# Moving a division to GpSimd, a second buffer for v and a new order of loads in a fused four-layer kernel

## The chip, the cores and the metric

The kernel runs on one core of a Trainium2 chip, as one program with one launch. The time is the device time of that program in microseconds (us). Before the change three runs took 3732.04, 3734.66 and 3744.95 us; the median, 3734.66 us, is what the change is measured against. The profile is of one further execution, whose span is 3730.0 us.

The core has five engines with their own in-order streams of instructions: TensorE (PE in the profile, its weight loads PEld), VectorE (DVE), ScalarE (ACT), GpSimd (POOL) and SyncE (SP), which issues most of the transfers here.[...]

## The reference, cut to what matters

Four layers follow each other on x of 4 images, 256 channels, 48 x 48 points, float32; each adds its result to x after a group norm. Layer 0 is an attention-weighted sum over 49 dilated taps, layers 1 and 2 are 3 x 3 convolutions with binarised and ternary weights. The change touches layer 3, a linear attention over square windows of three sizes:

```python
q = sigmoid(einsum('bchw,oc->bohw', x, Wq))        # 8 heads of 32 channels
k = sigmoid(einsum('bchw,oc->bohw', x, Wk))
v = einsum('bchw,oc->bohw', x, Wv)
v = v / maximum(norm(v, axis=1), 1e-12)            # per head
Ik, Ikv = integral(k), integral(k (x) v)           # two-dimensional running sums
for w in (1, 2, 4):                                # windows of 48, 24, 12 points
    wk, wkv = box(Ik, 48 // w), box(Ikv, 48 // w)  # sums over the window
    attn = einsum('bdhw,bdfhw->bfhw', q, wkv)
    norm = einsum('bdhw,bdhw->bhw', q, wk)
    outs.append(attn / (norm + 1e-6))              # <- the division
out = einsum('bchw,oc->bohw', concatenate(outs), Wout) + bout
```

## The kernel before

Layer 3 does not use running sums for `wkv`. It works in blocks: an image b, one half of the heads ct (four heads of 32 channels are 128 partitions) and eight rows of queries rb. Six row blocks, two halves and four images make 48 blocks, counted i = 0 to 47 in the order image, half, row block. A block goes over tiles of keys (a row block a, a third of the columns c): TensorE makes the scores of a tile, VectorE, ScalarE and GpSimd copy them out of PSUM under the masks of the three windows, and two tiles later TensorE adds up scores times v.

```python
LAG = 2
stream = [(i, a, c, ...) for i, (b, ct, rb) in enumerate(order) for n, (a, c) in enumerate(tiles_of(rb))]
for n in range(len(stream) + LAG):
    if n < len(stream):                       # tile n
        if at == 0: begun(i)
        ss = [blocks[i].scores(pr, a, c) for pr in range(NPR)]
        ahead.append(blocks[i].masked(a, c, ss))
        if at == 5: midway(i)                 # in the last heads: start(prepare(i))
    if n >= LAG:                              # tile n - 2
        if at == 0:
            if i >= 2: until(("done", i - 2))
            blocks[i].begin()                 # zeroes the accumulators
        for wi in (1, 0, 2): blocks[i].sums(wi, a, c, sms)
        if last: done(i)                      # finish(i) comes into turn
    advance()                                 # one step of all side jobs
```

All else runs as side jobs, Python generators that emit a few instructions at each step and say with `yield n` that they want to be called again n steps later: the next image's projections, running sums of k, norms, and the preparation and the end of blocks. The order in which they are called is the order of the instructions on each engine. `until` takes steps without emitting a tile.

```python
free = {"xr": 2, "xn": 2, "kt": 2, "sq": 2, "vt": 1, "cs": 1, "o": 1, "rc": 2, "res": 2}
FETCH = 4                                     # steps given to a transfer

def tiles_of(rb):                             # rows near rb and far ones take turns
    tiles = [(a, c) for a in sorted(range(NRB), key=lambda a: abs(a - rb)) for c in (1, 0, 2) if seen(0, a, rb)]
    near = [t for t in tiles if seen(NW - 1, t[0], rb)]
    far = [t for t in tiles if t not in near]
    both = min(len(near), len(far))
    return [t for pair in zip(near, far) for t in pair] + near[both:] + far[both:]

def prepare(i):                               # for blocks of the last heads
    yield from wait_for(("norm", b, rb))
    yield from take("o")
    o = op.tile([P, NW, NB], F32, tag="o", name="o", bufs=1)
    sync.dma_start(out=o..., in_=o_d[b][rb])  # the first heads' sums, stored earlier
    ...                                       # res: the rows of x
    for t in range(NCT):                      # one over the norms of both halves
        yield from take("rc")
        rc = op.tile([P, NW, NB], F32, tag="rc", name="rc")
        for g in range(HG):
            sync.dma_start(out=rc[g * D : (g + 1) * D]..., in_=r_d[b][rb, t * HG + g]....partition_broadcast(D))
        rcs.append(rc)
    prepared[i] = o, res, rcs

def finish(i, stage):
    yield 1
    if ct == 0:                               # first heads: store the sums
        sync.dma_start(out=o_d[b][rb], in_=stage...); made.add(("done", i)); return
    while i not in prepared: yield 1
    o, res, rcs = prepared.pop(i)
    os = (o, stage)
    for t, src in enumerate(os):              # the division, six times 128 x 384
        for wi in range(NW):
            dve.tensor_mul(src[:, wi], src[:, wi], rcs[t][:, wi])
            yield 1
        free["rc"] += 1
    for mo in range(NCT):                     # output: two accumulations on one bank
        yield from bank(2)
        ps = ps_m.tile([P, 512], F32, tag="st", name="out_ps")[:, 0:NB]
        for kt in range(NW * NCT):
            pe.matmul(ps, wout_sb[:, kt, mo * P : (mo + 1) * P], os[kt % NCT][:, kt // NCT, :], ...)
        yield 1
        dve.scalar_tensor_tensor(xs, ps, bout_sb[:, mo : mo + 1], xs, ALU.add, ALU.add)
    made.add(("done", i)); free["o"] += 1
    ...                                       # store res to the output
```

`v` of the class `Projection` makes v of one row block in three pieces, normalises it and stores it. It runs for image 0 beside image 3's layers 1 and 2, and for the other images beside the attention of the image before. The class has its tiles from a pool `scr` with two buffers for each name, unless `bufs` says otherwise:

```python
if c == 0:
    yield from take("vt")
    self.vs[g] = (self.scr.tile([P, NKC, HEADS, D], F32, tag="vt", name="vt", bufs=1), ...)
...                                           # matmuls into ps
act.copy(vt[:, c], ps)
...                                           # squares (GpSimd), sums (VectorE); for the last piece:
dve.tensor_mul(vt, vt, r...)
sync.dma_start(out=v_d[b][:, a * NKC : (a + 1) * NKC], in_=vt)
free["vt"] += 1
```

The attention stage begins with the loads for block 0; one call issues one row block of keys and one of v:

```python
qs = {0: load_q(*order[0])}
for a in range(seen_first):                   # 0, 1, 2, 3
    load_kv(0, 0, a)
```

Of the kernel before, what the change touches and what calls it, by code (L numbers as in the profile page):

```python
# [12 lines left out]
F32 = mybir.dt.float32  # L13
# [8 lines left out]
P = 128  # L22
# [52 lines left out]
HEADS, D = 8, 32  # L75
WINDOWS = (1, 2, 4)
NW = len(WINDOWS)
HALVES = [H // w // 2 for w in WINDOWS]
KC = P // RB
NKC = W // KC  # L80
# [65 lines left out]
def conv_preact_kernel(  # L146
# [53 lines left out]
    pe, dve, act, pool, sync = (  # L200
        InOrder(tc, e) for e in (nc.tensor, nc.vector, nc.scalar, nc.gpsimd, nc.sync)
    )
# [53 lines left out]
    def wait_for(*keys):  # L256
        while not made.issuperset(keys):
            yield 1

    def bank(steps):  # L260

        nonlocal bank_free
        while step < bank_free:
            yield 1
        bank_free = step + steps


    free = {"xr": 2, "xn": 2, "kt": 2, "sq": 2, "vt": 1, "cs": 1, "o": 1, "rc": 2, "res": 2}

    FETCH = 4  # L270

    def take(what):
        while free[what] == 0:
            yield 1
        free[what] -= 1
# [11 lines left out]
    class Projection:  # L287
# [84 lines left out]
        def v(self, g, a, c):  # L372
            b = self.b
            while g not in self.xn or (c > 0 and g not in self.vs):
                if g in self.left:
                    return
                yield 1
            if c == 0:
                yield from take("vt")
                self.vs[g] = (  # L380
                    self.scr.tile([P, NKC, HEADS, D], F32, tag="vt", name="vt", bufs=1),
                    self.scr.tile([P, NKC, HEADS], F32, tag="ss", name="ss"),
                )
            vt, ss = self.vs[g]
            yield from bank(1)
            ps = self.ps_tile()[:, 0:C].rearrange("p (h d) -> p h d", d=D)
            for ct in range(NCT):
                pe.matmul(
                    ps,
                    self.xn[g][:, ct, c, :],  # L390
                    proj["v"][:, ct, :],
                    start=(ct == 0),
                    stop=(ct == NCT - 1),
                )
            self.used(g)
# [3 lines that stand above are left out]
            yield from take("sq")  # L399
            sq = self.scr.tile([P, HEADS, D], F32, tag="sq", name="sq")  # L400
            pool.tensor_mul(sq, vt[:, c], vt[:, c])
            yield 2
            dve.tensor_reduce(ss[:, c, :], sq, AX.X, ALU.add)
            free["sq"] += 1
            if c < NKC - 1:
                return

            n = NKC * HEADS
            t = ss.rearrange("p k h -> p (k h)")
            r, s, u = (small.tile([P, n], F32, tag=f"{x}{n}", name=x) for x in ("vr", "vs", "vu"))  # L410
            dve.tensor_scalar_max(t, t, 1e-24)
            yield 1
            act.activation(s, t, AF.Sqrt)
            yield 1
            dve.reciprocal(r, s)
            dve.tensor_mul(u, t, r)
            dve.tensor_mul(u, u, r)
            dve.tensor_scalar(u, u, -0.5, 1.5, ALU.mult, ALU.add)
            dve.tensor_mul(r, r, u)
            dve.tensor_mul(  # L420
                vt,
                vt,
                r.rearrange("p (k h) -> p k h", h=HEADS)
                .unsqueeze(3)
                .to_broadcast([P, NKC, HEADS, D]),
# [4 lines that stand above are left out]
            made.add(("v", b, a))  # L430
# [21 lines left out]
    with (  # L452
# [26 lines left out]
        stage, owed = len(POINTS), 0.0  # L479
# [901 lines left out]
        with tc.tile_pool(name="wst", bufs=1) as wst:  # L1381
# [18 lines left out]
            for ct in range(NCT):  # L1400
                for k0, k1 in TAPS:
# [3 lines left out]
                    else:  # L1405
                        pool_, tag = {
                            (0, 0): (xp, "x1_0"),
                            (0, 2): (xp, "x1_1"),
                            (1, 0): (wst, "raw1"),
                            (1, 2): (wst, "raw"),  # L1410
                        }[ct, k0]
# [70 lines left out]
    with (  # L1482
# [179 lines left out]
        def load_q(b, ct, rb):  # L1662
            qs = qp.tile([P, RB, W], F32, tag="qs", name="qs")
            sync.dma_start(
                out=qs.rearrange("p r w -> p (r w)"),
                in_=q_d[b][ct * P : (ct + 1) * P, rb * NB : (rb + 1) * NB],
            )
            return qs
# [158 lines left out]
        def seen(wi, a, rb):  # L1827
            r0, r1 = rows_seen(wi, a, rb)
            return r0 < r1

        def tiles_of(rb):


            tiles = [
                (a, c)
                for a in sorted(range(NRB), key=lambda a: abs(a - rb))
                for c in (1, 0, 2)
                if seen(0, a, rb)
# [6 lines that stand above are left out]
        def prepare(i):  # L1845

            b, ct, rb = order[i]
# [3 lines that stand above are left out]
            sync.dma_start(out=o.rearrange("p w n -> p (w n)"), in_=o_d[b][rb])  # L1851
            yield from take("res")
            res = scr.tile([P, NCT, RB, W], F32, tag="res", name="res")
            sync.dma_start(
                out=res,
                in_=x3_d[b][:, rb * RB : (rb + 1) * RB, :].rearrange("(ct p) r w -> p ct r w", p=P),
            )
            rcs = []
            for t in range(NCT):
# [3 lines that stand above are left out]
                    sync.dma_start(  # L1863
                        out=rc[g * D : (g + 1) * D].rearrange("p w n -> p (w n)"),
                        in_=r_d[b][rb, t * HG + g]
                        .rearrange("w n -> (w n)")
                        .partition_broadcast(D),
                    )
                rcs.append(rc)
            prepared[i] = o, res, rcs  # L1870

        def finish(i, stage):


            b, ct, rb = order[i]
            yield 1
            if ct == 0:
                sync.dma_start(out=o_d[b][rb], in_=stage.rearrange("p w n -> p (w n)"))
                made.add(("done", i))
                return  # L1880
            while i not in prepared:
                yield 1
            o, res, rcs = prepared.pop(i)
            os = (o, stage)
            for t, src in enumerate(os):
                for wi in range(NW):
                    dve.tensor_mul(src[:, wi], src[:, wi], rcs[t][:, wi])
                    yield 1
                free["rc"] += 1
            for mo in range(NCT):  # L1890
                yield from bank(2)
                ps = ps_m.tile([P, 512], F32, tag="st", name="out_ps")[:, 0:NB]
                for kt in range(NW * NCT):
                    pe.matmul(
                        ps,
                        wout_sb[:, kt, mo * P : (mo + 1) * P],
                        os[kt % NCT][:, kt // NCT, :],
                        start=(kt == 0),
                        stop=(kt == NW * NCT - 1),
                    )  # L1900
                yield 1
                xs = res[:, mo].rearrange("p r w -> p (r w)")
                dve.scalar_tensor_tensor(
                    xs, ps, bout_sb[:, mo : mo + 1], xs, ALU.add, ALU.add
                )
            made.add(("done", i))
            free["o"] += 1
            yield 1
            free["res"] += 1
            sync.dma_start(  # L1910
                out=out[b, :, rb * RB : (rb + 1) * RB, :].rearrange("(ct p) r w -> p ct r w", p=P),
                in_=res,
            )

        kvs, prepared = {}, {}
# [12 lines left out]
        seen_first = HALVES[0] // RB + 1  # L1928
        until(("q", 0, 0, 0), *((what, 0, *at) for a in range(seen_first) for what, at in (("k", (0, a)), ("v", (a,)))))
        qs = {0: load_q(*order[0])}  # L1930
        for a in range(seen_first):
            load_kv(0, 0, a)


# [53 lines left out]
        for n in range(len(stream) + LAG):  # L1988
            if n < len(stream):
                i, a, c, at, last = stream[n]  # L1990
# [6 lines left out]
            if n >= LAG:  # L1997
                i, a, c, at, last = stream[n - LAG]
# [57 lines left out]
```

## Time and profile before

| | us |
|---|---|
| span of the profiled execution | 3730.0 |
| TensorE matmuls busy | 3284.1 |
| VectorE busy | 2494.9 |
| GpSimd busy | 1528.0 |
| ScalarE busy | 1067.4 |
| division of the first heads' sums, `o<-o,rc`, 72 on VectorE | 68.1 |
| division of the last heads' sums, `stage<-stage,rc`, 72 on VectorE | 58.5 |
| a multiplication of the same shape on GpSimd, `nhi<-nhi,nq` (mean of 144) | 1.055 |

Every operation is recorded through one helper line, L142, so groups are told apart by their tiles: `s` are scores, `sm` masked scores, `acc` the sums in PSUM, `stage` the sums in SBUF, `o` the first heads' sums loaded back, `rc` one over the norms, `out_ps` the output accumulation, `nhi` and `nlo` the norms' operands, `vt` v before its store, `ks` and `vs` keys and v as loaded for the attention. A row of groups gives count, busy time, mean duration and the idle time of the engine just before. A row of waits says who waited for whom, the total in us, how often, and the longest.[...] The row of a stretch of time gives its bounds and length, the busy time and number of instructions of PE, PEld, DVE, ACT and POOL, the clock granted to TensorE as a share of full speed, the DMA engines' busy share, and GB/s.

### The profile page before, as it was taken

What the parts mean: (1) busy time and instruction counts of PE and PEld (TensorE: products, weight loads), DVE (VectorE), ACT (ScalarE), POOL (GpSimd) and SP (SyncE); (2) the same over time, 40 slices, a digit from 0 to 9 for tenths busy, and PEclk for the clock granted to TensorE, in tenths of its full rate; (3) what the DMA queues carried; (4) which work ended last, traced back from release to release, by engine and by line L of the source; (5) the groups of instructions that cost most, each with busy time, mean ns of one, the idle gap of its engine ahead of it and who ended that gap; (6) DMA issues with size and microseconds to landing.
All of it is one profiled execution on the core that took longest, in us unless ns stands there. A gap on an engine that the chain in (4) does not pass through costs nothing. (4 is left out here: it accounts for less than half of the span.)

```text
span 3730.0 us, 69121 instructions
## 1 busy us (share of the span) xinstructions
PE 3284.1 (88%) x26498; PEld 1873.8 (50%) x26498; DVE 2494.9 (67%) x5059; ACT 1067.4 (29%) x2085; POOL 1528.0 (41%) x2184
## 2 busy tenths in 40 slices
PE   3689998998996788988899888999999899999998
PEld 2467686686784664433334333344444344444443
DVE  7876587586583266778667466866577866666665
ACT  0012111111114422443222334333344422333331
POOL 0000120120030024788765476866366766344442
PEclk9789999999997899999899999999999999999999
DMA  7745333324314323345344253434222444200222
GB/s 251 225 143 184 101 108 120 105 98 125 107 65 124 117 70 98 119 140 168 105 133 134 74 151 109 154 99 136 75 94 87 153 124 124 70 31 31 65 60 60
DMA packets 373020, 423.04 MB, mean 113 GB/s; under 512 B 129076, under 2 KB 328532, under 8 KB 371540
## 3 DMA queue, kind: packets, MB, share of 16 engines
q1 hardware_dynamic: 371491, 416.32, 36.2%
q8 instruction: 211, 3.46, 0.4%
q0 software_dynamic: 144, 1.52, 0.2%
q14 instruction: 118, 0.96, 0.1%
q10 hardware_dynamic: 1056, 0.79, 0.1%
HBM read 288.79 MB, written 131.25 MB: 113 GB/s over the span
## 5 line engine op out<-in xcount | busy, mean ns | idle before, releaser
L142 DVE TENSOR_TENSOR sm<-s,masks 128x112 f32<-128x112 f32 (+10 forms) x2592 | 1149.2, 492 | 704.7 <-ACT sm L142 297.1
L142 POOL TENSOR_TENSOR sm<-sm,masks 128x432 f32<-128x432 f32 (+14 forms) x1152 | 883.1, 788 | 900.9 <-ACT sm L142 397.5
L142 ACT COPY sm<-s 128x528 f32<-128x528 f32 (+2 forms) x1152 | 588.3, 534 | 1423.0 <-PE s L142 1281.9
L142 PE MATMUL s<-qs,ks 32*128 32x320 f32 (+3 forms) x5760 | 859.7, 499 | 127.8 <-ACT sm L142 65.2
L142 PE MATMUL acc<-sm,vs 128*32 128x384 f32 (+18 forms) x13440 | 879.5, 384 | 21.5 <-POOL sm L142 21.2
L142 PEld LDWEIGHTS s<-qs,ks 32*128 32x128 f32 x5760 | 372.0, 185 | 558.3 <-DVE sm L142 225.1
L142 PE MATMUL cv<-vx,wt 128*128 128x288 f32 x2080 | 561.1, 426 | 92.5 <-DVE vx L142 50.7
L142 PEld LDWEIGHTS acc<-sm,vs 128*32 128x32 f32 x13440 | 355.0, 110 | 555.0 <-issue 327.0
L142 PEld LDWEIGHTS cv<-vx,wt 128*128 128x128 f32 x2080 | 403.5, 198 | 213.8 <-issue 55.2
L142 POOL MEMSET v<- 128x16 f32 (+1 forms) x120 | 18.5, 214 | 722.1 <-DVE vx L142 628.5
L142 PE MATMUL cv<-v,wl 128*128 128x384 f32 x1152 | 222.2, 352 | 24.3 <-DVE x L142 9.2
L142 PEld LDWEIGHTS cv<-v,wl 128*128 128x128 f32 x1152 | 212.7, 193 | 34.0 <-issue 15.8
L142 POOL TENSOR_TENSOR pt<-pt 128x144 f32<-128x144 f32 x336 | 180.4, 537 | 22.3
L142 POOL TENSOR_TENSOR v<-l2v,v 128x384 fp32r<-128x384 f32 x96 | 109.0, 1164 | 127.0 <-ACT v L142 118.3
L142 POOL TENSOR_TENSOR nhi<-nhi,nq 128x384 f32<-128x384 f32 x144 | 147.9, 1055 | 0.0
L142 PE MATMUL cv<-pad,wl 128*128 128x384 bf16 x864 | 143.1, 327 | 0.0
L142 PE MATMUL out_ps<-o,wout_sb 128*128 128x384 f32 x288 | 123.7, 512 | 11.2 <-DMA rc<-r_d 5.7
L142 DVE TENSOR_TENSOR pt<-cs 128x384 f32<-128x384 f32 x144 | 119.2, 827 | 0.0
L142 PE MATMUL out_ps<-stage,wout_sb 128*128 128x384 f32 x288 | 118.6, 494 | 0.5 <-DVE stage L142 0.5
L142 DVE TENSOR_TENSOR vx<-v 128x868 f32<-128x868 f32 x112 | 115.3, 1055 | 0.5
L142 PE MATMUL proj_ps<-wv_sb,xn 128*128 128x256 f32 x288 | 88.3, 434 | 29.3 <-ACT vt L142 19.3
L142 PEld LDWEIGHTS <-wl 128*128 128x128 bf16 x864 | 83.8, 97 | 59.1 <-issue 0.4
(162 smaller groups left out, 2881.3 us busy)
## 6 DMA issues: line engine op xcount, KB each, us to landing
wt<-wt SPq DMA_DIRECT2D x48, 768.0 KB
kb_d<-pt SPq DMA_DIRECT2D x48, 576.0 KB
rc<-r_d SPq DMA_DIRECT2D x192, 144.0 KB
nhi<-kb_d SPq DMA_DIRECT2D x120, 192.0 KB
nlo<-kb_d SPq DMA_DIRECT2D x88, 192.0 KB
o_d<-stage SPq DMA_DIRECT2D x24, 576.0 KB
o<-o_d SPq DMA_DIRECT2D x24, 576.0 KB
wl<-wl_d SPq DMA_DIRECT2D x16, 768.0 KB
```

What stands on the lines that cost most here:

```text
L142: return lambda *args, **kwargs: self.tc.keep_in_program_order(op(*args, **kwargs))
```

## The change

It has three parts. The division of the first heads' sums goes from VectorE in `finish` to GpSimd in `prepare`, which runs in the second half of the block: it is meant to be over when the block ends, and to leave VectorE to the masks. The tile `vt` gets the pool's two buffers, so that the next v can be copied while one is stored; its token stays at 1. And the first block's keys are loaded in the order in which its tiles use them: row blocks 0, 2, 1, 3.

```diff
-                    self.scr.tile([P, NKC, HEADS, D], F32, tag="vt", name="vt", bufs=1),
+                    self.scr.tile([P, NKC, HEADS, D], F32, tag="vt", name="vt"),
@@ prepare
                 rcs.append(rc)
-            prepared[i] = o, res, rcs
+
+            yield FETCH
+            for wi in range(NW):
+                pool.tensor_mul(o[:, wi], o[:, wi], rcs[0][:, wi])
+                yield 2
+            free["rc"] += 1
+            prepared[i] = o, res, rcs[1]
@@ finish
-            o, res, rcs = prepared.pop(i)
+            o, res, rc = prepared.pop(i)
             os = (o, stage)
-            for t, src in enumerate(os):
-                for wi in range(NW):
-                    dve.tensor_mul(src[:, wi], src[:, wi], rcs[t][:, wi])
-                    yield 1
-                free["rc"] += 1
+            for wi in range(NW):
+                dve.tensor_mul(stage[:, wi], stage[:, wi], rc[:, wi])
+                yield 1
+            free["rc"] += 1
@@ start of the attention
-        for a in range(seen_first):
+        for a in dict.fromkeys(a for a, _ in tiles_of(0)):
             load_kv(0, 0, a)
```

## The prediction, written before the changed kernel was run

> **What bounds the kernel now.** I read the page's totals first, then the busy time by stage, then the waits of the attention stage, then single windows of the timeline. The totals:
>
> ```profile
> PE 3284.1 (88%) x26498; PEld 1873.8 (50%) x26498; DVE 2494.9 (67%) x5059; ACT 1067.4 (29%) x2085; POOL 1528.0 (41%) x2184
> ```
>
> TensorE is the busiest engine, but 88% is a mean over stages. I cut the attention stage into its halves: first heads of image 0 (1430 to 1726), last heads of image 0 (to 2040), and so on; each half has six blocks, and blocks are counted from 0 to 47. The columns are TensorE, weight loads, VectorE, ScalarE and GpSimd busy, then clock, DMA share, GB/s:
>
> ```profile
> 1160.00:1420.00 260.00, 200.42 (x1000) 152.41 (x998) 115.80 (x282) 96.56 (x171) 41.10 (x79) 0.86 0.31 99
> 1726.00:2040.00 314.00, 277.81 (x2598) 122.45 (x2598) 216.63 (x427) 85.54 (x172) 207.22 (x280) 0.95 0.45 130
> 2368.00:2647.00 279.00, 264.27 (x2602) 118.81 (x2600) 191.10 (x395) 85.28 (x172) 177.07 (x229) 0.99 0.43 123
> 2942.00:3221.00 279.00, 263.74 (x2600) 118.68 (x2598) 190.92 (x395) 84.95 (x172) 176.80 (x228) 0.99 0.43 124
> 3451.00:3708.00 257.00, 248.90 (x2508) 114.42 (x2506) 168.72 (x353) 77.86 (x157) 104.71 (x140) 1.00 0.21 59
> ```
>
> Two things matter. In the last-heads halves of images 1, 2 and 3 TensorE is busy 95 to 97% at nearly full clock: there, taking work from VectorE cannot buy more than the 3 to 5% of idle. And two stretches are loose: the first projection (1160 to 1420; TensorE 77% at a clock of 0.86) and image 0's last heads, 35 us longer than the same work of image 1. Only there can anything sizable be won or lost. The waits of the attention stage:
>
> ```profile
> PEld s L142 <- DVE sm L142: 225.1, 346, 4.5
> PEld acc L142 <- POOL sm L142: 86.7, 145, 5.1
> PE s L142 <- DVE sm L142: 47.5, 98, 3.9
> PE acc L142 <- POOL sm L142: 21.2, 23, 4.6
> PEld out_ps L142 <- DVE o L142: 6.2, 1, 6.2
> ```
>
> Nearly all of the weight-load waits are hidden under running matmuls; the rows of PE itself are what counts: 47.5 us behind VectorE's masks, 21.2 us behind GpSimd's. For the division `o<-o,rc` itself TensorE waited once, at the very end. So the division is not a wait to be removed; it only delays masks behind it on VectorE.
>
> [...] the same VectorE division took 495 ns at least, 916 in the median. [...] `nhi<-nhi,nq`, the same shape there, takes 1055 ns, against that undisturbed 495. [...] after the 5.66 us wait near the end, pairs of output matmuls take 1.65 us, later 0.81. So a stall of several microseconds costs more than its length.[...]
>
> **The change part by part.**
>
> *Two buffers for v.* With one, the first copy into `vt` of each group waits until the store of the group before has landed. The answer for `vt` between 1150 and 1420, idle times in us and how often:
>
> ```profile
> DMA v_d<-vt: 21.1, 5
> ...
> PEld proj_ps L142: 26.9, 7
> PE proj_ps L142: 23.2, 5
> ```
>
> The first line is ScalarE's idle time before those copies, the others TensorE's wait for `vt`. In the timeline the five are 5.1, 4.2, 2.9, 1.3 and 7.6 us, and ScalarE and TensorE both take their work in order, so each holds all that follows. TensorE's gaps at these places are 6.9 us (of which 5.1 is the store), 2.5, 1.1, about 0 and 7.3 (some 6.9): 5.1 + 2.5 + 1 + 0 + 6.9 = 15.5 us. The clock over the two big ones is 0.74 and 0.66, so the slow matmuls after them may give 2 to 5 us more; some is given back to waits next in line (stores of `sg`, loads of x), which I put at 3. **Minus 16 us.** The token that counts v's buffers in the program stays at 1, so the order of instructions does not move. In the attention stage no copy into `vt` waits for its store, so nothing there.
>
> *Order of keys.* The first block takes tiles of rows 0, 2, 0, 2, 0, 2, 1, 3; the loads came 0, 1, 2, 3. The second tile's wait (start, length, engine, what, idle before it):
>
> ```profile
> 1424.52 0.66 PEld L142 LDWEIGHTS s<-qs,ks 32*128 32x128 f32 x8 [7.76 <-issue]
> 1424.55 1.78 PE L142 MATMUL s<-qs,ks 32*128 32x384 f32 x8 [6.64 <-DMA ks<-k_d]
> ```
>
> Its keys are issued at 1417.2 and used at 1424.5. In the new order they are issued one pair (1.0 us) earlier, and are no longer behind the 384 KB of the pair for row 1, which is 1.4 us at the some 270 GB/s moved in those microseconds. The rest of the wait is the stage's other loads (768 KB of output weights) and stays. **Minus 1.5 us.**
>
> *Division moved.* Off VectorE: 24 blocks of 3, 72 x 948 ns = 68 us. Onto GpSimd: 72 x 1055 ns = 76 us. The 72 divisions of `stage` stay on VectorE. Neither sum is on the path by itself.
> - In tight halves (images 1 to 3, 18 blocks) TensorE idles about 2 us per block, while blocks of image 3 without a division and output idle 1.1 to 1.6. The division can be charged with about 0.4 us: 18 x 0.4 = 7. **Minus 6.**
> - Image 0's last heads: GpSimd is the late one. The three longest TensorE gaps waiting for GpSimd there, 4.3, 2.8 and 4.6 us (at 1771, 1836, 1894), end when a mask comes out behind three `nhi` operations of norms in a row (3.1 us). Counting the program's steps, the new multiplications fall at the start of blocks 8 and 9, step 186 to 190 and 203 to 207, and so into those stretches, where GpSimd is busy 19.3 to 19.8 of 20 us. VectorE loses its divisions in the same stretches (1.28, 0.84, 1.34 us by one block's timeline). I take **plus 3**.
> - Steps. The division must now wait four steps for its loads and takes six more, and `prepared` comes only after it. Counted through the generators, block 11 is done at step 267 instead of 261, and block 13, which must not begin before that, waits 4 steps in which no tile of attention is emitted; images 2 and 3 likewise, 12 steps in all by the end. In such steps both output accumulations stand back to back on one PSUM bank, with VectorE's add between (TensorE's gap for it at the end of the kernel: 1.3 us), behind three divisions of `stage` at some 0.8 us. I take 2.7 us each: **plus 8.**
> - The end. The last block's `o` is fetched once the block before has let go of the single buffer, one step later than now (one scores and sums more, some 2 us). Then GpSimd's three at 1.05 us run beside VectorE's three at 0.5 instead of six on VectorE: about even. **Plus 2.**
>
> Sum: -16 - 1.5 - 6 + 3 + 8 + 2 = -10.5, so 3734.7 - 10.5 = **3724 us**.
>
> **Rivals.**
> - *VectorE bounds the attention stage, and 68 us off it come back nearly whole.* For it: 225 us of weight loads waiting for VectorE's masks. Against: TensorE busy 95% and more in three of four images, and image 3's blocks 1 to 4 of the last heads are 7.9 to 8.4 us longer than the same blocks of its first heads, where 24 output matmuls at 0.32 us take 7.7, so the divisions cost next to nothing. It would make 3660 to 3690.
> - *GpSimd becomes the bound.* For it: its waits in image 0[...]. If it hit nine blocks of images 0 and 1 with 4 us each: 3745 to 3760. Against: 60% busy or less in later images, and a lag of two tiles between scores and sums (some 6 us).
> - *The v stores were hidden anyway*, the waits only move to the next in-order wait. Then v gives 3 to 5 us and the total is about 3736.
>
> **Range and chances.** The v term may be -4 to -25, image 0 -10 to +12, the steps 0 to +15. They are mostly independent; added as spreads, about 18 us each side, and before's own runs span 13 us: 3702 to 3742. Two per cent is 75 us, more than all of the idle time that the changed parts touch; so within 2% at 0.97.
>
> **What would show it.** Right: `vt` has no wait for `v_d<-vt` any more and the stretch from 1160 to the first scores is 12 to 20 us shorter; the new `o<-o,rc` group is on GpSimd, x72, near 1055 ns; tight halves 279 us give or take 3; a gap before the second block of images 1, 2 and 3; the second tile's wait for keys at 4 to 5.5 us. Wrong: if the tight halves shorten by over 8 us each, VectorE was the bound; if TensorE's wait for GpSimd's masks grows well beyond 21.2 us, the second rival; if the first projection takes as long as before, the third.

## The result and the profile after

The changed kernel takes 3677.93 us (median of four runs, 3669.71 to 3689.4) where the kernel before, on the same chips, takes 3737.36: a ratio of 0.9842, with a 95% interval of 0.9808 to 0.9875. That is some 59 us less where 10 were predicted, and below the range of 3702 to 3742. The profile is of the slowest of the four runs, with a span of 3687.6 us; the totals, as before (TensorE, weight loads, VectorE, ScalarE, GpSimd):

```profile
PE 3266.4 (89%) x26498; PEld 1876.3 (51%) x26498; DVE 2445.5 (66%) x4987; ACT 1069.5 (29%) x2085; POOL 1578.3 (43%) x2256
```

The 72 divisions have moved: VectorE has 72 operations fewer, GpSimd 72 more. Their groups, with count, busy time, mean ns and the idle time before them:

```profile
L142 POOL TENSOR_TENSOR o<-o,rc 128x384 f32<-128x384 f32 x72 | 73.2, 1018 | 13.0 <-DMA rc<-r_d 13.0
L142 DVE TENSOR_TENSOR stage<-stage,rc 128x384 f32<-128x384 f32 x72 | 60.6, 844 | 9.3 <-DMA rc<-r_d 9.3
```

1018 ns was foreseen as 1055. The stretches: the first projection, the first heads of image 1, and the last heads of images 1 and 2 (columns as before):

```profile
1170.00:1404.00 234.00, 193.71 (x1000) 147.39 (x998) 113.24 (x272) 95.92 (x170) 41.35 (x78) 0.89 0.33 107
2021.00:2339.00 318.00, 282.50 (x2669) 124.85 (x2666) 212.60 (x443) 126.72 (x248) 220.58 (x306) 0.96 0.41 126
2339.00:2610.00 271.00, 256.94 (x2594) 117.74 (x2592) 178.75 (x379) 85.34 (x171) 183.09 (x236) 1.00 0.41 118
2907.00:3178.00 271.00, 256.92 (x2598) 117.73 (x2592) 178.40 (x378) 85.22 (x170) 182.97 (x236) 1.00 0.41 119
```

The last two were 279 us, "give or take 3" foreseen. TensorE's idle time in them hardly moved (15 us before, 14 now); its *busy* time fell by 7 us. Only 8 matmuls (one projection, 2.1 us from start to start) left these halves; the rest is the same matmuls, recorded shorter. From start to start the scores' matmuls take 141 ns each instead of 145, the sums' (with the zeroing ones) 70 instead of 71 or 72, while the page gives a scores' matmul a duration of some 498 ns. So a wait of up to some 350 ns (498 less 141) between two of them shows as busy time; that the 7 us are such waits is inferred from these numbers, not shown. Of the 8 us of each half, from start to start, 2.1 are the projection, 2.5 to 3 the sums, as much again the scores, and the rest the norms.

What the profile does show as TensorE's waits behind VectorE's and GpSimd's masks was 47.5 and 21.2 us over the attention; it is now:

```profile
PE s L142 <- DVE sm L142: 32.1, 57, 4.0
PE acc L142 <- POOL sm L142: 27.5, 26, 5.4
```

To place the difference I cut both traces at the same instructions: a convolution matmul late in image 3's layer 0 (nothing before it is touched by the change), the first scores, and the first zeroing matmul of each block.

| us | before | after | difference |
|---|---|---|---|
| start to late in layer 0 of image 3 (same code) | 1097.0 | 1107.7 | +10.7 |
| from there to the first scores (v) | 319.2 | 295.7 | -23.5 |
| first scores to first sums (keys) | 13.1 | 8.7 | -4.4 |
| image 0: first heads, last heads | 296.4, 314.7 | 295.8, 313.3 | -2.0 |
| image 1: first heads, last heads | 327.7, 279.1 | 317.5, 270.9 | -18.4 |
| image 2: first heads, last heads | 294.6, 279.3 | 297.4, 271.2 | -5.3 |
| image 3: first heads, last heads without the last block | 229.7, 224.3 | 230.1, 222.5 | -1.4 |
| last block | 54.8 | 56.6 | +1.8 |

The first row is no effect of the change: over all profiles of this case the same mark lies between 1093.7 and 1107.7 us. With it the two profiles differ by 42 us, without it by 53, inside the interval of the whole (47 to 72 us). In the rows of the attention the changed kernel's two profiles agree to within 2.2 us, so a single profile tells larger differences apart. Where no ratio is given below, the kernel ran once.

### The profile page after: what moved, and what is told of

Same layout as the page of the kernel before. It is cut to its first block, busy times and chain, and to the rows that moved or that the text cites. A ratio compares the mean times of both kernels' runs of the same rounds, so it can differ in the third digit from the quotient of the medians.

```text
span 3687.6 us, 69067 instructions
## 1 busy us (share of the span) xinstructions
PE 3266.4 (89%) x26498; PEld 1876.3 (51%) x26498; DVE 2445.5 (66%) x4987; ACT 1069.5 (29%) x2085; POOL 1578.3 (43%) x2256
## 5 line engine op out<-in xcount | busy, mean ns | idle before, releaser
L142 POOL TENSOR_TENSOR sm<-sm,masks 128x432 f32<-128x432 f32 (+14 forms) x1152 | 865.7, 773 | 821.5 <-ACT sm L142 347.5
L142 PE MATMUL s<-qs,ks 32*128 32x320 f32 (+3 forms) x5760 | 847.5, 498 | 111.4 <-ACT sm L142 67.0
L142 PE MATMUL acc<-sm,vs 128*32 128x384 f32 (+18 forms) x13440 | 879.0, 383 | 27.5 <-POOL sm L142 27.5
L142 DVE SCALAR_TENSOR_TENSOR x<-cv,alpha,x 128x384 f32<-128x384 f32 x144 | 83.9, 610 | 45.6 <-PE cv L142 45.3
```

The source lines that it names most:

```text
L142: return lambda *args, **kwargs: self.tc.keep_in_program_order(op(*args, **kwargs))
```

## The theories

**Theory 1:** VectorE's load is what counts. With 68 us off it, masks come sooner.

**Theory 2:** the place in the program counts. The late division lets a block's end, with its two outputs on the single PSUM bank for side jobs, fall on later steps; projections, norms and running sums then come elsewhere among the tiles.

**A third, the rival of the prediction:** GpSimd becomes the bound. For v, the rival is that the waits only move on.

## The experiments

**Second buffer for v alone.**

```diff
 # kernel before
-    self.scr.tile([P, NKC, HEADS, D], F32, tag="vt", name="vt", bufs=1),
+    self.scr.tile([P, NKC, HEADS, D], F32, tag="vt", name="vt"),
```

> The kernel before with the second buffer for v alone. If the stores of v were waits on the path, the stretch from the end of image 3's layer 0 to the first scores gets some 20 us shorter (the changed kernel's profile has 23.5 us less there together with nothing else that touches it), and the attention after it takes as long as before to within 1 us per half. Prediction's size: 16 us. Rival (the waits only move on): 3 to 5 us. Total about 3715.

Measured: 3713.31 us, ratio 0.9937 (0.9921 to 0.9954). The stretch up to the first scores takes 292.6 us, 26.6 less; the attention's halves are those of before to within 3 us. Answer for `vt` in this kernel, idle times first:

```profile
ACT vt L142: 95.8, 13
DVE ss L142: 16.2, 3
PE proj_ps L142: 3.4, 3
...
PEld proj_ps L142: 10.3, 4
PE proj_ps L142: 8.4, 3
```

The line `DMA v_d<-vt` is gone, and nothing of its size has come in its place; TensorE's own waits for `vt` fall from 23.2 to 8.4 us. Following equal matmuls through both traces, from start to start, shows where the 26.6 us come from: some 15 us at the three gaps where TensorE had waited for a store (5.2, 2.7 and 7.3 us), 7 us because matmuls close behind the gaps run faster (the clock granted in the 8 us behind them in the kernel before is 0.61, 0.50 and 0.50; over the whole stretch it is 0.86 there, 1160 to 1420, and 0.92 here, 1160 to 1395), another 7 us in a stretch that begins 37 us after the second gap, and about 3 us given back. Timeline of TensorE in that stretch, the kernel before and then this one, the same 24 matmuls of layer 0:

```profile
1245.22 5.25 PE L142 MATMUL ap<-seen,xT 120*128 120x120 f32 x24
```

```profile
1234.82 2.81 PE L142 MATMUL ap<-seen,xT 120*128 120x120 f32 x24
```

The clock granted around them in the kernel before is 0.55 (1240 to 1250); in the changed kernel, where the same 24 start at 1241.4 and take 2.81 us too, it is 1.00 (1234 to 1244). The buffer alone does not decide this: the kernel below with the division left out at its new place has two buffers for v and waits for no store of v, and yet:

```profile
1237.39 5.25 PE L142 MATMUL ap<-seen,xT 120*128 120x120 f32 x24
```

Of the twelve kernels here with two buffers for v, two run this stretch slowly, and the whole way to the first scores takes 292 to 300 us in the twelve. That the second 7 us follow from the gaps is not shown.

**The division alone.**

```diff
 # changed kernel, v and keys as before
-    self.scr.tile([P, NKC, HEADS, D], F32, tag="vt", name="vt"),
+    self.scr.tile([P, NKC, HEADS, D], F32, tag="vt", name="vt", bufs=1),
-        for a in dict.fromkeys(a for a, _ in tiles_of(0)):
+        for a in range(seen_first):
```

> The kernel before with the division's move alone (GpSimd, in the preparation). The first projection takes as long as before. In the attention: last heads of images 1 and 2 shorter by 8 us each, first heads of image 1 shorter by 10 us, all other halves within 3 us, as in the changed kernel; together some 25 us less. If the prediction's working held instead, it would be 7 us more. Total about 3710.

Measured: 3714.33 us, ratio 0.9944 (0.9928 to 0.9961). The first projection is back at 320.3 us; the five halves from the last heads of image 0 to those of image 2 take 312.8, 316.6, 271.1, 295.7 and 272.7 us, together some 26 less than before. The parts add up: 0.9937 x 0.9944, with 4.4 us for the keys, gives 0.987, inside the interval of the whole, near its upper end.

**Only the engine: the early division on VectorE.**

```diff
 # changed kernel, in prepare
-                pool.tensor_mul(o[:, wi], o[:, wi], rcs[0][:, wi])
+                dve.tensor_mul(o[:, wi], o[:, wi], rcs[0][:, wi])
```

> The changed kernel, but the three early multiplications of each block go to VectorE, at the same steps of the program; only the engine differs. Theory 1 (VectorE's load is what counts: 68 us off it come back in part): the last heads of images 1 and 2 go back up from 271 to about 277 us each. Theory 2 (the place in the program counts: the block's end has three multiplications fewer between sums and output, and side jobs fall on other steps): they stay at 271 to 273. First heads of image 1: theory 1 back towards 328, theory 2 stays near 317.

Measured: 3690.4 us; first heads of image 1 319.0, last heads 274.7 (image 1) and 272.2 (image 2):

```profile
2016.00:2335.00 319.00, 282.91 (x2668) 123.80 (x2664) 213.88 (x444) 126.80 (x248) 218.57 (x303) 0.96 0.40 125
2907.00:3179.00 272.00, 257.43 (x2592) 117.82 (x2592) 187.61 (x393) 85.29 (x171) 171.83 (x220) 1.00 0.41 118
```

VectorE has the divisions again (187.6 us instead of 178.4 in the second row), and the five halves take only some 8 us more than with GpSimd (1479 to 1471). Theory 1 falls as the main cause.

**Only the steps without tiles.**

```diff
 # kernel before with v and keys changed
                     if i >= 2:
                         until(("done", i - 2))
+                    if i in (13, 25, 37):
+                        for _ in range(4):
+                            advance()
```

> The kernel before with second v buffer and new order of keys; the division stays on VectorE at the block's end, and before blocks 13, 25 and 37 begin, four steps are taken without a tile, as the late division causes in the changed kernel. Theory 2 for the first heads (the empty steps shift the projections against the tiles): first heads of image 1 at about 317 us instead of 328, last heads of images 1 and 2 2 us shorter by the projection that moved out of them. Theory 1: first heads of image 1 stay at 328 or get 3 us longer. Prediction: 2.7 us longer at each of the three places.

Measured: 3711.98 us; first heads of images 1 and 2 334.5 and 303.0, last heads 273.2 and 274.6. So the first heads lose 7 and 8 us, but the last heads win 6 and 5, of which 2.1 are a projection that now falls into the first heads. Over both halves empty steps by themselves cost about 1 us in image 1 and 4 in image 2, and nothing in the first heads of image 3 (229.6 us): together less than the 8 of the prediction. Theory 2 in the form "the empty steps do it" is wrong for the first heads.

**The same ends of blocks, all divisions on VectorE.**

```diff
 # kernel before with v and keys changed, in prepare
+            yield FETCH + 2
             prepared[i] = o, res, rcs
```

> All six divisions stay on VectorE at the block's end, as in the kernel before (with second v buffer and new order of keys), but the preparation reports itself six steps later without doing anything, so that every block's end and its output fall on the step on which they fall in the changed kernel, to within one. Theory 2 (the place of the block's end among the side jobs counts): the first heads of image 1 at 315 to 322 us, last heads of images 1 and 2 at 272 to 275. Theory 1 (VectorE's load at the block's end counts): first heads of image 1 near 328, last heads near 279.

Measured: 3698.59 us; first heads of image 1 319.8, last heads 276.3 and 272.9:

```profile
2016.00:2336.00 320.00, 280.42 (x2663) 125.08 (x2661) 212.67 (x444) 126.29 (x248) 217.05 (x303) 0.96 0.40 122
2912.00:3185.00 273.00, 258.59 (x2600) 117.43 (x2592) 189.22 (x394) 85.27 (x170) 172.75 (x221) 1.00 0.40 116
```

No engine has a multiplication less than before, and 8 of the 10 us of image 1's first heads are there. TensorE's wait behind VectorE's masks over the attention has fallen from 47.5 us almost to the changed kernel's 32.1:

```profile
PE s L142 <- DVE sm L142: 34.7, 64, 3.9
```

Theory 2 holds, for about half of the gain. Counted in scores' matmuls ahead of a block's first output, the changed kernel moves the last end of images 0, 1 and 2 six tiles later, and every other end by at most one tile, earlier or later; here they lie within one tile of that. Part of what the last heads win is only moved: a projection now falls into the first heads, and those of image 2 take 300.0 us instead of 294.6.

**Only one end of a block.**

```diff
 # kernel before with v and keys changed, in finish
+            if i == 11:
+                yield 5
             o, res, rcs = prepared.pop(i)
```

> The kernel before with second v buffer and new order of keys, all divisions on VectorE at their old place; one thing differs: the end of block 11 (image 0's last) waits five steps, so that the next image's first projections get the single PSUM bank ahead of its two outputs. Theory 2: first heads of image 1 fall from 328 to 316 to 321 us, and what follows shifts a little. Theory 1: they stay at 328.

Measured: 3701.93 us; first heads of image 1 318.1:

```profile
2021.00:2339.00 318.00, 278.19 (x2661) 124.33 (x2660) 212.63 (x443) 126.30 (x249) 216.81 (x302) 0.97 0.39 121
```

Five steps at one block of 48 are worth the 10 us. The last heads after it stay slow, 277.8 and 281.4 us. The first 111 us of that half in the kernel before and 102 in this one, waits (total, times, longest):

```profile
PEld proj_ps L142 <- ACT sg L142: 7.5, 3, 5.2
...
PE proj_ps L142 <- ACT sg L142: 5.9, 2, 4.5
...
ACT sg L142 <- DMA q_d<-sg: 3.9, 1, 3.9
PE norm_ps L142 <- ACT sg L142: 3.7, 1, 3.7
```

```profile
PEld proj_ps L142 <- ACT sg L142: 2.7, 1, 2.7
...
PE proj_ps L142 <- ACT sg L142: 2.4, 1, 2.4
```

Before, block 11's outputs take the bank first and push image 1's projections together behind them; a sigmoid then waits for the store of `sg`, and TensorE for the sigmoid, 4.5 us. The 3.7 us of `norm_ps` have another cause: that sigmoid stands on ScalarE behind a square root and two table loads (`ACT_TABLE_LOAD`) of 1.28 us each. With the outputs later, a q and two k projections go first, and neither wait is left.

**The division left out at its old place.** The first heads' sums stay undivided.

```diff
 # kernel before with v and keys changed, in finish
-                    dve.tensor_mul(src[:, wi], src[:, wi], rcs[t][:, wi])
+                    if t > 0:
+                        dve.tensor_mul(src[:, wi], src[:, wi], rcs[t][:, wi])
                     yield 1
```

> The kernel before with second v buffer and new order of keys, and the first heads' sums not divided at all: the 72 multiplications are left out, their steps stay. It shows what VectorE's 68 us cost where they stood. Theory 1: last heads of images 1 and 2 fall from 279 to about 271 us each, first heads of image 1 from 328 towards 318. Theory 2: last heads 276 to 278, first heads of image 1 stay at 325 to 328.

Measured: 3699.5 us; last heads 278.6 and 280.8, first heads of image 1 321.1:

```profile
2009.00:2330.00 321.00, 280.12 (x2658) 122.97 (x2656) 207.35 (x439) 126.01 (x246) 213.29 (x294) 0.96 0.38 116
2904.00:3185.00 281.00, 266.02 (x2606) 119.20 (x2600) 179.69 (x381) 85.13 (x172) 173.47 (x229) 0.99 0.43 123
```

VectorE is as free in the second row as in the changed kernel (180 us), and the half takes 281 us and not 271. Nor does TensorE wait much less behind VectorE's masks over the attention:

```profile
PE s L142 <- DVE sm L142: 45.2, 96, 3.9
```

In the slow first heads of image 1 relief does help, by some 7 us.

**GpSimd at the old place.**

```diff
 # kernel before with v and keys changed, in finish
-                    dve.tensor_mul(src[:, wi], src[:, wi], rcs[t][:, wi])
+                    (pool if t == 0 else dve).tensor_mul(src[:, wi], src[:, wi], rcs[t][:, wi])
```

> The kernel before with second v buffer and new order of keys, the first heads' division on GpSimd but at its old place, at the block's end and on the old steps: the engine alone. Theory 1 (VectorE is relieved of the same 68 us as in the changed kernel): last heads of images 1 and 2 at 271 to 273 us, first heads of image 1 at about 318. Theory 2: last heads 277 to 281, first heads of image 1 325 to 330. Rival of GpSimd as the bound: last heads of image 0 over 320.

Measured: 3718.55 us; last heads of image 0 320.3, first heads of image 1 329.7, last heads 281.4 and 281.0:

```profile
2926.00:3207.00 281.00, 265.86 (x2606) 119.19 (x2600) 179.85 (x381) 85.13 (x172) 188.00 (x244) 0.99 0.43 123
```

The engine alone gains nothing; in image 0, where GpSimd is busy for up to 19.8 of 20 us (1820 to 1840 in the kernel before), it costs 3 to 6 us.

**The division left out at its new place.** Again the first heads' sums stay undivided; all steps remain.

```diff
 # changed kernel, in prepare
-                pool.tensor_mul(o[:, wi], o[:, wi], rcs[0][:, wi])
                 yield 2
```

> The changed kernel with the early multiplications left out (the first heads' sums are not divided), all steps as they are: what the 76 us on GpSimd cost. If they are hidden: all halves within 2 us of the changed kernel's, last heads of images 1 and 2 at 270 to 271. If GpSimd pays: last heads of image 0 some 5 us shorter than 313, and the end of the kernel 3 to 5 us shorter, because the last division stands alone there.

Measured: 3680.02 us; last heads of image 0 308.1, of images 1 and 2 271.0 and 271.3, last block 55.5. So GpSimd's work costs 5 us in image 0 and is hidden in the tight halves. The expected gain at the end did not come: there the loads set the pace (the division of `stage` waits 8.9 us for `rc`).

**Two buffers for the first heads' sums.** The last block's `o` is fetched only when the block before has let go of it. With v's second buffer kept to the first projection there is room for a second `o`.

```diff
 # changed kernel
-    free = {..., "o": 1, ...}
+    free = {..., "o": 2, ...}
-            o = op.tile([P, NW, NB], F32, tag="o", name="o", bufs=1)
+            o = op.tile([P, NW, NB], F32, tag="o", name="o")
                 rcs.append(rc)                # inside the loop over both halves
+                if t == 0:
+                    yield FETCH
-            yield FETCH                       # after the loop
```

> The changed kernel with two buffers for the first heads' sums as well (v's second buffer in the attention stage makes room for it; the division of o starts before the last heads' norms are loaded). Nothing waits for the single buffer any more, the block's end comes on its earliest step again, and no steps without a tile are taken. Theory 2 (place): what was won is lost again although GpSimd still does the division: first heads of image 1 back at 325 to 329 us, last heads of images 1 and 2 at 276 to 279. Theory 1 or the tidy view (fewer waits are better): 317 and 271 or less. Both: the last block, from its first sums to the end, at 46 to 49 us instead of 56.6, because the division is done before the block ends.

Measured: 3717.08 us; first heads of image 1 321.0, last heads 290.1 and 289.1, last block 46.1. The end is 10 us shorter, and the tight halves are some 18 us *longer*, more than theory 2 had said. The ends now come one to three tiles earlier than in the kernel before. Then the same kernel, with every block's end but the last held to the steps of the changed one:

```diff
 # in finish, added to the kernel above
+            if i + 1 < len(order) and rb > 0:
+                yield (0, 4, 3, 2, 4, 7)[rb]
             o, res, rc = prepared.pop(i)
```

> As the run before, two buffers for o, but every block's end except the last is held back to exactly the step it has in the changed kernel. Theory 2: all halves as in the changed kernel to within 2 us (first heads of image 1 at 317, last heads of images 1 and 2 at 271), the last block at 46 to 49 us instead of 56.6, so 8 to 10 us less than the changed kernel in all: about 3668 against its 3678.

Measured: 3663.93 us (3658.72 to 3665.56), ratio 0.9796 (0.9770 to 0.9823); last heads 271.1 and 273.0, last block 46.6. The windows of image 2's last heads, first with the early ends, then with the held ones, and the last block of the second:

```profile
2929.00:3218.00 289.00, 269.34 (x2601) 119.42 (x2600) 180.23 (x381) 85.30 (x173) 188.99 (x246) 0.99 0.43 122
```

```profile
2890.00:3163.00 273.00, 258.41 (x2596) 118.00 (x2592) 179.11 (x379) 85.24 (x170) 185.08 (x238) 0.99 0.42 122
3616.00:3662.00 46.00, 40.19 (x337) 19.21 (x336) 21.42 (x42) 8.15 (x17) 13.41 (x18) 0.99 0.09 31
```

16 us of this half, and 19 of image 1's, hang on the steps of the ends alone; 2.1 of them are a projection that the later ends leave to the first heads. In the early form TensorE's norm matmuls wait for GpSimd longer (idle before them, us and times, early and then held):

```profile
POOL nhi L142: 11.1, 16
```

```profile
POOL nhi L142: 5.9, 4
```

From start to start they take 285 ns each instead of 183, together 6 us of the 16; the sums' and zeroing matmuls take another 6 (74 ns instead of 71, with 1692 of them). The changed kernel beside it:

> The changed kernel once more on this chip, to compare with the run before: 3670 to 3690, every half of the attention within 2 us of its first profile, layers 0 to 2 up to 10 us apart.

Measured: 3685.77 us (3681.09 to 3693.83), ratio 0.9861 (0.9827 to 0.9895); the halves are those of its first profile to within 2.2 us. The version with two buffers and held ends thus beats both kernels, the changed one by some 22 us, of which its profile shows 11 in the last block and 9 in the last heads of image 0 and the first of image 1.

## Why the prediction was wrong

The sum of the five halves that the division touches, from the last heads of image 0 to those of image 2, puts the runs in one table (us; the kernel before and the one with v alone give the first number's spread). For the division's terms there, -6, +3 and +8, the prediction had +5; the changed kernel's profile shows -25 (1495 to 1470).

| where the first heads' division is done | ends of blocks as before | ends as in the changed kernel |
|---|---|---|
| VectorE, at the end | 1495 to 1500 | 1484 |
| VectorE, early | | 1479 |
| GpSimd | 1508 (at the end) | 1469 to 1472 (early) |
| left out | 1490 | 1462 |

- **Steps: this step failed, and in sign.** It priced only what empty steps cost, +8. With empty steps alone the sum is 1502, 2 to 7 more than before, so that price was no worse than a little high. But the moved ends also changed who gets the single bank first, as image 1's start shows; that the norms and running sums meet other masks as well is argued, not shown. All together it is not +8 but about -14 (1498, the middle of 1495 to 1500, to 1484), and -29 where no division stands in the way (1490 to 1462). I had counted the steps on which ends fall, and asked only for the idle time there, not what the side jobs behind them would meet.
- **v: mechanism right, one term too small.** 15.5 us of waits were about 15. The term that was mis-sized is the clock: 2 to 5 us foreseen, 7 measured close behind the gaps and 7 in the later stretch; 3 given back, as foreseen. In the later stretch the 24 matmuls take 5.25 us at a granted clock of 0.55 in the kernel before and 2.81 us in the one with v's second buffer alone, and in the 30 us ahead of it in the kernel before no two matmuls had started more than 2.1 us apart. What lets the clock fall there stays open. Minus 16 became minus 23.5 in the changed kernel's profile, and minus 19 to 28 over the twelve.
- **Keys: right in kind.** The second tile's wait fell from 6.64 to 2.65 us and the stretch by 4.4, not 1.5: the rest of that wait was not only the other loads.
- **VectorE's relief: about right.** Predicted -6; leaving the work out at the old place gives -5 to -10 (1495 to 1500 against 1490). But it does not simply add: at the new ends, from VectorE at the end to nothing, it is -22 (1484 to 1462). The claim under it was wrong: that TensorE's idle share bounds what a tight half can win. The halves lost 7 us of *busy* time.
- **GpSimd: its cost was +9 and not +3** (1462 to 1471), 5 us of it in image 0, where it was looked for. Its load was also read too low: "60% busy or less in later images" was 65 and 63% in the halves of image 1 and 63% in the last heads of image 2. The early place on GpSimd is nevertheless worth -13 against all six on VectorE at the end (1484 to 1471).
- **The end: right**, +1.8 for +2, with GpSimd's division waiting 12 us for its loads.

Of the rivals, "VectorE bounds the attention" named a total (3660 to 3690) that the measurement fell into, and its sign, tight halves more than 8 us shorter, was just met (8.2 and 8.1), for a reason that the runs don't bear out: with all divisions on VectorE and the ends moved, half of the gain is there, and with the division gone but the ends unmoved the tight halves stay at 278.6 and 280.8 us. GpSimd as the bound is not borne out either: TensorE's wait for its masks grew only from 21.2 to 27.5 us. Why a moved end helps has been shown for one place, image 1's start. For the tight halves it stays open: the steps decide, and which matmuls slow down is known, but empty steps alone, with the ends within a tile of their old places, already bring them to 273.2 and 274.6 us.

## What to carry to other kernels

In a program whose side jobs are emitted by counted steps, an operation's new place can shift everything that shares a bank, a buffer or an engine's order with it; before pricing the engine, list which job gets the shared bank next in either order. Test it by moving the end alone, without the work: here `yield 5` at one block gave 10 us. And a wait that is taken away should be priced with the slow matmuls close behind it (here 7 us beside 15).

## What the runs showed that was not expected

- TensorE's busy time can hold waits: the same halves lost 7 us of it with 8 of 2600 matmuls moved away. Times from start to start (145 to 141 ns for scores) show what durations (498 ns) hide.
- A resource added can cost: a second buffer for `o` brought the blocks' ends forward and made the tight halves 18 us longer, until the ends were held back by 2 to 7 steps.
- TensorE ran at about half pace not only close behind gaps of 3 to 8 us (granted clock 0.61, 0.50 and 0.50), but also in a stretch (0.55; 24 matmuls in 5.25 us instead of 2.81) before which no two matmuls had started more than 2.1 us apart for 30 us. Slow matmuls cost about as much as the gaps themselves, 14 us against 15.
